# Two changes of order in a two-layer kernel: the weight folding among the experts, and a context product in the last two units

## The chip, the cores and the metric

The kernel runs on one core of a Trainium2 chip. The metric is the device time of one execution in microseconds (us); the median of the runs is what two kernels are compared by. The core has five engines with a queue each: TensorE (PE, with its weight loads shown as PEld), VectorE (DVE), ScalarE (ACT), GpSimd (POOL), and SyncE (SP), which here issues most of the transfers (DMAs). In what follows a line number such as L869 is a line of the kernel before.

## What is computed

Two layers over x of shape (4, 512, 512) in float32. Each adds to x an attention and a feed-forward part of the normed x:

```python
x = L0_attn_hidden_states
xn = _layernorm(x, axis=-1)
x = x + _L0_attn_ref(xn, ...) + _L0_ffn_ref(xn, ...)
xn = _layernorm(x, axis=-1)
x = x + _L1_attn_ref(xn, ...) + _L1_ffn_ref(xn, ...)
```

The change lies in the second layer alone. Its feed-forward part has four experts (E = 4); row n of a batch goes through expert n mod 4:

```python
x4 = x.reshape(B, G, E, H)
gu = jnp.einsum('bgeh,ehd->bged', x4, gate_up_proj)
gate, up = (gu[..., :I], gu[..., I:])
inter = jax.nn.silu(gate) * up
out = jnp.einsum('bgei,eih->bgeh', inter, down_proj)
```

Its attention works on compressed keys and queries, with 16 heads of 128 (H, D) and a rotation of half of each head:

```python
c_kv = hidden_states @ W_DKV + b_DKV
k = (c_kv @ W_UK + b_UK).reshape(b, s, H, D)
v = (c_kv @ W_UV + b_UV).reshape(b, s, H, D)
c_q = hidden_states @ W_DQ + b_DQ
q = (c_q @ W_UQ + b_UQ).reshape(b, s, H, D)
q_r = q @ W_QR
k_r = k @ W_KR
...
q = q.at[..., :RD].set(rope(q_r))
k = k.at[..., :RD].set(rope(k_r))
scores = jnp.einsum('bqhd,bkhd->bhqk', q, k) / jnp.sqrt(jnp.float32(D))
probs = jax.nn.softmax(scores, axis=-1)
ctx = jnp.einsum('bhqk,bkhd->bqhd', probs, v).reshape(b, s, H * D)
return ctx @ W_O + b_O
```

## The kernel before

**Order of instructions.** The program is written with tiles; a scheduler decides in which order the instructions of one engine stand, by the data that they need and by its own estimate of times. Each engine then works through its queue strictly in the order laid down, and waits where an instruction's data is not there. `tc.keep_in_program_order(ins)` adds an edge from the instruction that stands before it in the program on the same engine: the instruction can't be placed ahead of that one. In the attention's part nearly all instructions are held in this way, through a small helper `pin`.

**Stages.** The first layer fills the time up to some 976 us. Then come the four experts (to about 1150 us), and then the attention of the second layer in 64 units of one head and one batch.

**The experts (`hidden`, `returned`).** Expert e has a weight of 512 x 1024 for gate and up (`gu_e`, 2 MB) and one of 512 x 512 (`dn_e`). `hidden(e)` goes through four blocks of 128 columns. A block is done by products of 128 x 256 with fewer multiplications than the plain form (Strassen's scheme in Winograd's form): seven products, `a11`, `a12`, `s2`, `s1`, `s3`, `s4`, `a22`, of two matmuls each. They write into two tiles of PSUM, `epg` and `epu`. Three of the products go on adding to the same half of `epg`, called x, and ScalarE has to copy x out between them: L997 after `a11`, L999 after `s2`, L1003 after `s3`; L1001 copies `epu`. VectorE then makes the two sums `g` (tile `esg`: L1007 and L1008), ScalarE applies Silu to them (L1009), VectorE makes one more sum (L1010, tile `hold`) and the two products into `inter` (L1014). VectorE also makes the left operands of a later block from `gu` (L957 to L960, tile `s_ops`) and the right operands of the next expert (L946 to L949, tile `t_ops`). The copies share one tile, so the copy L997 of a block stands on ScalarE behind the Silu of the block before.

`gates(e)` loads `gu_e`; there are two buffers, and the load of `gu_2` waits until expert 0 has read `gu_0`. `returned(e)` multiplies `inter` with `dn_e` and adds to y (L1028, L1035).

**The folding (`fold`).** The rotation's matrices and the value projection are multiplied into the projections once for each group of four heads, by a generator that works in steps. It is run for group 0 among the experts and for groups 1 to 3 within the attention. A step i of it

- multiplies the transposed block of step i - 1 with W_QR or W_KR (`pw`, L864) and copies it to the weight (L865),
- transposes the loaded block on VectorE (`wt`, L869),
- loads the next block (`raw`, L875).

For group 0 `raw` and `wt` have one buffer each. The blocks are raw_0 to raw_4. At the end four products `pvo` (L882, copied by L883) make the folded output weight from rows `ow` of W_O (L855, two buffers), and VectorE sums these rows into `bo_part` (L886, L888). The first step, which only loads raw_0, is taken after expert 1's `hidden` in program order, one step in each block of experts 2 and 3, and one after expert 2. Called among the experts, `fold` gets no `pin`, and its default leaves every instruction to the scheduler:

```python
def fold(w, hg, wk, psum, bufs, pin=lambda ins: ins, ahead=1, rows=nc.sync):
```

**The attention's loop.** Unit i makes its queries and keys (`pk`, L1116, and `pq`, L1124, rotated on VectorE and GpSimd), the scores `sc` (L1134) and softmax of the unit before, whose probabilities are transposed on VectorE in blocks (`tt`, L1163) and set in place by 16 transfers (`prT`, L1194). The context product `pc` (L1202) is three units behind; ScalarE copies it to `ctxT` (L1204). When four heads of a batch have their context, the output product is made by seven products of Strassen's scheme again, split in four parts by a generator `outputs`:

- part 1: px = a11 b11, added to y
- part 2: p2 = a12 b21; px goes on with s2 t2; p2 and px are added to y
- part 3: p5 = s1 t1; px goes on with s3 t3; three additions to y
- part 4: p3 = s4 b22; px goes on with a22 t4; two additions to y, and for the last group the stores

px lies in one PSUM bank of its own; the next addition into it has to wait until VectorE has read the content before (L1266). p2, p5, p3, pk, pq and pc take turns in three banks (`ps_pj`). Of the 64 units one part is made in each; in the last turns of the loop (i = 63 and i = 64) two, because no unit comes after them. In the profile p2, p5 and p3 all have the name p. After the loop, `project_out` (L1302) makes the output of the last batch plainly, with the last two contexts `pc_next` and `pc_last` between.

The loop's part in question (i is the unit's number, nu is 64):

```python
for _ in range(1 if i < nu - 1 else 2):
    next(outs, None)
if i >= 3:
    hg, b, h = units[i - 3]
    context(probs.pop(i - 3), b, cs[hg, b], h, f"{i - 3}")
    if h == HPG - 1:
        outs = outputs(hg, b, ws[hg], cs[hg, b])
```

Of the kernel before, what the change touches and what calls it, by code (L numbers as in the profile page):

```python
# [55 lines left out]
def trunk_kernel(ctx: ExitStack, tc: tile.TileContext, a: dict, out: bass.AP):  # L56
    nc = tc.nc
# [48 lines left out]
    with ExitStack() as px:  # L106
        one = px.enter_context(tc.tile_pool(name="b_one", bufs=1))
        wk = px.enter_context(tc.tile_pool(name="b_wk", bufs=2))
# [10 lines left out]
        def psum():  # L119
            return ps_pj.tile([P, 512], F32, tag="pj", name="pj")  # L120
# [119 lines left out]
        k1, q1, rows = {}, {}, {}  # L240
# [582 lines left out]
    buq = lat.tile([P, H], F32, tag="b_UQ", name="b_UQ")  # L823
    lv = lat.tile([P, B, E, KVC], F32, tag="lv", name="lv")

# [14 lines left out]
        w["vo"] = pool.tile([P, HPG, HS], F32, tag="vo", name=f"vo_{hg}", bufs=1)  # L843
        return w

    def fold(w, hg, wk, psum, bufs, pin=lambda ins: ins, ahead=1, rows=nc.sync):

        heads = slice(hg * HPG, (hg + 1) * HPG)
        for nm, src in zip(ups, up_srcs):
            nc.sync.dma_start(out=w[nm][:, :, :RD], in_=src.rearrange("p (h d) -> p h d", h=H)[:, heads, :RD])  # L850
        raws, turned, ows = {}, {}, {}

        def output_rows(h):
            ows[h] = wk.tile([P, HS], F32, tag="ow", name=f"ow_{hg}_{h}", bufs=2)
            rows.dma_start(out=ows[h], in_=a["W_O"][(hg * HPG + h) * D : (hg * HPG + h + 1) * D, :])  # L855

        n = len(up_srcs)
        for i in range(n + 1 + ahead):
            k = i - ahead - 1
            if 0 <= k < n - 1:  # L860
                wt, wr, to = turned.pop(k), wqr if k else wkr, w[ups[k]]
                pw = psum(f"pw_{hg}_{i}").rearrange("p (h d) -> p h d", h=HPG)[:, :, :RD]
                for h in range(HPG):
                    pin(nc.tensor.matmul(pw[:, h, :], lhsT=wt[:, h, :], rhs=wr, start=True, stop=True))  # L864
                pin(nc.scalar.copy(to[:, :, RD:], pw))  # L865
            if 0 <= i - ahead < n:
                t = turned[i - ahead] = wk.tile([P, HPG, P], F32, tag="wt", name=f"wt_{hg}_{i - ahead}", bufs=1)
                pin(
                    nc.vector.transpose(  # L869
                        out=t.rearrange("p h c -> p (h c)"), in_=raws.pop(i - ahead).rearrange("p h c -> p (h c)")  # L870
                    )
                )
            if i < n:
                raw = raws[i] = wk.tile([P, HPG, P], F32, tag="raw", name=f"raw_{hg}_{i}", bufs=bufs)
                nc.sync.dma_start(out=raw, in_=blocks_d[i][:, heads, :])  # L875
            if i - n - ahead + 1 >= 0:
                output_rows(i - n - ahead + 1)
            yield
        wt = turned.pop(n - 1)
        for h in range(HPG):  # L880
            pv = psum(f"pvo_{hg}_{h}")
            pin(nc.tensor.matmul(pv, lhsT=wt[:, h, :], rhs=ows[h], start=True, stop=True))  # L882
            pin(nc.scalar.copy(w["vo"][:, h, :], pv))  # L883
            hh = hg * HPG + h
            if hh == 0:
                pin(nc.vector.tensor_scalar_mul(bo_part, ows[h], buv[:, :1]))  # L886
            else:
                pin(nc.vector.scalar_tensor_tensor(bo_part, ows[h], buv[:, hh : hh + 1], bo_part, ALU.mult, ALU.add))  # L888
            if h + 2 < HPG:
                output_rows(h + 2)  # L890
            if h == 1:
                yield
        if hg == NHG - 1:
            pb = psum("pbo")
            pin(nc.tensor.matmul(pb, lhsT=ones, rhs=bo_part, start=True, stop=True))
            pin(nc.vector.tensor_add(bo, pb, bo))

    with ExitStack() as px:
# [3 lines left out]
        wk = px.enter_context(tc.tile_pool(name="d_wk", bufs=2, reuse_waits="tile"))  # L902
# [181 lines left out]
    with ExitStack() as px:  # L1084
        wk = px.enter_context(tc.tile_pool(name="e_wk", bufs=2, reuse_waits="tile"))
# [1 line left out]
        ps_x = px.enter_context(tc.tile_pool(name="e_psx", bufs=1, space=PSUM))  # L1087
        ps_sc = px.enter_context(tc.tile_pool(name="e_pssc", bufs=4, space=PSUM))

        def pin(ins):  # L1090
            tc.keep_in_program_order(ins)
            return ins

        def rotate(t, ps, bias, trig, nm):

            mid = RD + HALF
# [118 lines left out]
        def rows_cols(t, qh, oh):  # L1215

            return t[:, 2 * qh : 2 * qh + 2, oh * half : (oh + 1) * half]

        def right_operands(w):
            vo, t = w["vo"], t_ops  # L1220
            b11, b12, b21, b22 = (vo[:, 2 * k : 2 * k + 2, o : o + half] for k in range(2) for o in (0, half))
            nc.gpsimd.tensor_sub(t[:, 0], b12, b11)
            nc.gpsimd.tensor_sub(t[:, 1], b22, t[:, 0])
            nc.gpsimd.tensor_sub(t[:, 2], b22, b12)
            nc.gpsimd.tensor_sub(t[:, 3], b21, t[:, 1])
            return dict(b11=b11, b21=b21, b22=b22, t1=t[:, 0], t2=t[:, 1], t3=t[:, 2], t4=t[:, 3])
# [28 lines left out]
        def outputs(hg, b, w, c):  # L1255

            if b == 0:
                ws_right[hg] = right_operands(w)
            r = ws_right[hg]

            def bank(pool, tag, nm):
                return pool.tile([P, 2, half], F32, tag=tag, name=f"{nm}_{hg}_{b}")

            def add(ps, qh, oh):
                t = rows_cols(y[b], qh, oh)
                pin(nc.vector.tensor_add(t, ps, t))  # L1266

            x = bank(ps_x, "px", "px")
            block_product(x, left_blocks(c)["a11"], r["b11"])
            add(x, 0, 0)  # L1270
            o = left_operands(c)
            yield
            p2 = bank(ps_pj, "pj", "p2")
            block_product(p2, o["a12"], r["b21"])
            block_product(x, o["s2"], r["t2"], False)
            add(p2, 0, 0)
            add(x, 0, 1)
            yield
            p5 = bank(ps_pj, "pj", "p5")
            block_product(p5, o["s1"], r["t1"])  # L1280
            block_product(x, o["s3"], r["t3"], False)
            add(p5, 0, 1)
            add(p5, 1, 1)
            add(x, 1, 1)
            yield
            p3 = bank(ps_pj, "pj", "p3")
            block_product(p3, o["s4"], r["b22"])
            block_product(x, o["a22"], r["t4"], False)
            add(p3, 0, 1)
            add(x, 1, 0)  # L1290
            if hg == NHG - 1:
                for e in range(E):
                    nc.sync.dma_start(out=rows_of(out, b)[:, e], in_=y[b][:, e])
            yield
# [23 lines left out]
        nu = len(units)  # L1318
        ws, cs, qk, probs = {}, {}, {}, {}
        folds, outs = iter(()), iter(())  # L1320
        ws[0] = w0
        for i in range(nu + 1):
            if i < nu:
                hg, b, h = units[i]
                if h == 0:
                    if b == 1 and hg + 1 < NHG:
                        ws[hg + 1] = group_tiles((lat, wk)[(hg + 1) % 2], hg + 1)
                        folds = fold(
                            ws[hg + 1],
                            hg + 1,  # L1330
                            wk,
                            lambda nm: ps_pj.tile([P, 512], F32, tag="pj", name=nm),
                            2,
                            pin,
                            2,
                            nc.gpsimd,
                        )
                        next(folds)
                    if i + HPG < nu:
                        cqs[units[i + HPG][:2]] = batch_latents(*units[i + HPG][:2])  # L1340
                    cs[hg, b] = wk.tile([P, HPG, L], F32, tag="ctxT", name=f"ctxT_{hg}_{b}")
                qk[i] = queries_keys(hg, b, h, ws[hg])
            if i == nu:
                last = list(probabilities(*qk.pop(i - 1), f"{i - 1}"))
            elif i == 1:
                head = list(probabilities(*qk.pop(0), "0"))
            elif i > 1:
                if i == 2:
                    probs[0] = turned_at_once(head, "head")
                probs[i - 1] = turn(softmax(*qk.pop(i - 1), f"{i - 1}"), f"{i - 1}")  # L1350
            for _ in range(1 if i < nu - 1 else 2):
                next(outs, None)
            if i >= 3:
                hg, b, h = units[i - 3]
                context(probs.pop(i - 3), b, cs[hg, b], h, f"{i - 3}")
                if h == HPG - 1:
                    outs = outputs(hg, b, ws[hg], cs[hg, b])
            if i % HPG != 0:
                next(folds, None)
            k = i - (nu - HPG * B)  # L1360
            if 0 <= k < HPG * B:
                b, e = divmod(k, HPG)
                nc.gpsimd.tensor_add(y[b][:, e, :], y[b][:, e, :], bo)
# [110 lines left out]
```

## Time and profile before

| what | value |
|---|---|
| median of 3 runs | 2060.4 us (2059.95 to 2061.85) |
| the profiled execution: time | 2058.69 us |
| its span, first to last instruction | 2056.9 us |
| TensorE busy, first layer (0 to 976 us) | 925.19 of 976.00 us |
| TensorE busy, experts (976 to 1150 us) | 160.58 of 174.00 us |
| TensorE busy, attention to unit 62 (1150 to 1994.8 us) | 838.37 of 844.80 us |
| TensorE busy, from unit 63 to the end (1994.8 to 2056.9 us) | 54.09 of 62.10 us |
| TensorE's granted clock in these four | 0.99, 0.96, 1.00, 0.97 |

The profile lists the instructions of one execution. A row of its view in order of time reads: start in us, busy us, engine, line, operation, out<-in, shapes, number of instructions (a matmul of float32 is listed as two); in brackets the idle time before it and what ended it. A row of its list of waits reads: engine and line that waited, what it waited for, us in total, number of times, longest. A row of a table by stretches of time reads: from:to, length, busy us (and number) of PE, PEld, DVE, ACT and POOL, the granted clock of TensorE (1.00 is full), the share of the DMA engines' time, GB/s.

### The profile page before, as it was taken

How to read it: one execution, taken by the hardware profiler on the slowest of the kernel's cores; microseconds unless marked ns; L12 is line 12 of the kernel's file. 1: busy time of each engine (PE TensorE's matmuls, PEld its weight loads, DVE VectorE, ACT ScalarE, POOL GpSimd, SP SyncE). 2: the span in 40 equal slices, each digit the busy share in tenths (PEclk: the TensorE clock that was granted, in tenths of full speed). 3: DMA queues.
4: the chain of work that ended last, by engine and by line, in shares of the span. 5: the costliest groups of instructions: out<-in, count | busy, mean ns of one | idle time of the engine just before them, and what ended most of it. 6: DMA issues, size and time to landing. Idle time of an engine off the chain costs nothing.

```text
span 2056.9 us, 30728 instructions
## 1 busy us (share of the span) xinstructions
PE 1978.2 (96%) x10502; PEld 1252.2 (61%) x10502; DVE 1301.4 (63%) x2720; ACT 866.9 (42%) x1765; POOL 588.6 (29%) x635
## 2 busy tenths in 40 slices
PE   8998999899999999998799999999999999999998
PEld 6776676767667776744677445555555555555554
DVE  5444666475755674744554487777777777777772
ACT  2233343334343443412222265555555555555552
POOL 5232333333332333320000132233223232344220
PEclk9999999999999999999899999999999999999999
DMA  6756566656364556663721144344434443333332
GB/s 165 207 147 180 132 193 156 169 142 186 116 186 126 157 172 169 196 200 117 262 73 56 46 105 115 91 113 110 108 94 114 102 114 89 94 96 94 99 91 82
DMA packets 338950, 270.89 MB, mean 132 GB/s; under 512 B 104043, under 2 KB 259884, under 8 KB 338156
## 3 DMA queue, kind: packets, MB, share of 16 engines
q1 hardware_dynamic: 323808, 254.36, 45.0%
q0 software_dynamic: 3488, 9.27, 1.4%
q10 hardware_dynamic: 11500, 5.32, 0.9%
q8 instruction: 84, 1.38, 0.3%
q14 instruction: 70, 0.57, 0.1%
HBM read 174.18 MB, written 34.87 MB: 102 GB/s over the span
## 4 chain that ended last, share of the span: by engine, by line
PE 45%; SPq 3%; DMA 2%; DVE 1%; ACT 1%; issue 0%; ACTq 0%; DVEq 0%
PE pc L1202 9%; PE sc L1134 9%; PE pq L1124 7%; PE px L1245 5%; PE p L1245 4%; PE epg L965 3%; PE epo L1028 3%; PE pk L1116 2%; SPq L1194 2%; PE epu L965 1%; PE po L1302 1%; PE pw L864 1%; PE pvo L882 1%; ACT prob L1139 1%; DMA y<-yd 1%
## 5 line engine op out<-in xcount | busy, mean ns | idle before, releaser
L1139 ACT ACTIVATE prob<-sc,mx 128x512 f32<-128x512 f32 x256 | 174.5, 684 | 160.7 <-DVE mx L1136 156.0
L1134 PE MATMUL sc<-kT,qT 96*128 96x512 f32 x512 | 230.6, 592 | 1.6 <-DVE prT_head L1183 1.3
L1202 PE MATMUL pc<-prT,lv 128*128 128x512 f32 x488 | 220.1, 594 | 0.7 <-DMA prT<-tt 0.7
L1163 DVE STREAM_TRANSPOSE tt<-prob 128x512 f32<-128x512 f32 x248 | 170.3, 706 | 55.1 <-ACT prob L1144 45.8
L1109 POOL TENSOR_TENSOR kT<-t_k,t_k 32x512 f32<-32x512 f32 x64 | 80.6, 1260 | 407.6 <-PE pq L1124 225.4
L117 PE MATMUL pf<-xT,wg 128*128 128x256 f32 x704 | 174.3, 390 | 13.5 <-DVE hid L478 7.3
L1144 ACT ACTIVATE prob<-prob,sm 128x512 f32<-128x512 f32 x256 | 176.6, 714 | 0.0
L1124 PE MATMUL pq<-cq,uq 128*128 128x512 f32 x384 | 175.3, 592 | 1.1 <-ACT ctxT L1204 1.1
L1134 PEld LDWEIGHTS sc<-kT,qT 96*128 96x128 f32 x512 | 96.8, 190 | 124.5 <-issue 119.4
L1136 DVE TENSOR_REDUCE mx<-sc 128x1 f32<-128x512 f32 x256 | 168.1, 677 | 6.2 <-PE sc L1134 4.2
L117 PE MATMUL pf<-xT,wu 128*128 128x256 f32 x704 | 170.4, 386 | 0.0
L117 PE MATMUL pd<-wd,hid 128*128 128x512 f32 x352 | 165.6, 600 | 1.0 <-DMA wd<-in_wd 0.7
L117 PEld LDWEIGHTS pf<-xT,wg 128*128 128x128 f32 x704 | 133.1, 193 | 39.9 <-DVE hid L478 9.4
L1202 PEld LDWEIGHTS pc<-prT,lv 128*128 128x128 f32 x488 | 92.8, 191 | 93.9 <-issue 89.6
L117 PEld LDWEIGHTS pf<-xT,wu 128*128 128x128 f32 x704 | 136.2, 194 | 19.6 <-issue 0.2
L478 DVE SCALAR_TENSOR_TENSOR hid<-pf,us,sg 128x256 f32<-128x256 f32 x88 | 41.7, 475 | 142.7 <-ACT sg L477 141.9
L1124 PEld LDWEIGHTS pq<-cq,uq 128*128 128x128 f32 x384 | 72.8, 190 | 93.4 <-issue 82.0
L314 POOL TENSOR_SCALAR sk<-k,m 128x256 f32<-128x256 f32 x64 | 61.0, 965 | 203.5 <-PE pz L117 190.4
L421 POOL TENSOR_SCALAR gh<-grad,m 128x256 f32<-128x256 f32 x64 | 62.6, 989 | 151.9 <-DVE grad L390 144.4
L117 PEld LDWEIGHTS pd<-wd,hid 128*128 128x128 f32 x352 | 63.6, 190 | 59.6 <-issue 44.8
L477 ACT ACTIVATE sg<-pf,gs 128x256 f32<-128x256 f32 x88 | 41.6, 474 | 131.7 <-PE pf L117 131.3
L1109 POOL TENSOR_TENSOR qT<-t_q,t_q 32x512 f32<-32x512 f32 x64 | 80.7, 1261 | 56.3 <-DVE t_q L1105 56.3
(301 smaller groups left out, 3512.2 us busy)
## 6 DMA issues: line engine op xcount, KB each, us to landing
prT<-tt SPq DMA_DIRECT2D x992, 64.0 KB, 2.0
wd<-in_wd SPq DMA_DIRECT2D x176, 256.0 KB, 3.0
wg<-in_wg SPq DMA_DIRECT2D x88, 256.0 KB, 2.8
wu<-in_wu SPq DMA_DIRECT2D x88, 256.0 KB, 3.2
cq<-lat_d SPq DMA_DIRECT2D x48, 256.0 KB, 3.9
rows<-rows SPq DMA_DIRECT2D x128, 66.0 KB, 2.2
kv<-rows SPq DMA_DIRECT2D x32, 264.0 KB, 4.3
gu<-in_gu SPq DMA_DIRECT2D x3, 2048.0 KB, 7.8
```

Source lines behind the costliest of these rows:

```text
L117: nc.tensor.matmul(out, lhsT=lhsT, rhs=rhs, start=start, stop=stop, skip_group_check=True)
L421: nc.gpsimd.tensor_scalar_mul(gh[:, :, h, :], g, m2[:, h : h + 1])
L965: nc.tensor.matmul(ps, lhsT=w[:, c, :], rhs=x[:, c], start=start and c == 0, stop=c == 1, skip_group_check=True)
L1109: nc.gpsimd.tensor_sub(t[RD:mid, :], t1[RD:mid, :], t2[RD:mid, :])
L1124: nc.tensor.matmul(pq, lhsT=w[f"uq{i}"][:, h, :], rhs=cqs[hg, b][:, i, :], start=(i == 0), stop=(i == nq - 1))
L1134: pin(nc.tensor.matmul(ps, lhsT=qT[:KQ, i * P : (i + 1) * P], rhs=kT[:KQ, :], start=True, stop=True))
L1136: pin(nc.vector.tensor_reduce(mx, ps, AX.X, ALU.max, negate=True))
L1139: pin(nc.scalar.activation(pr, ps, AF.Exp, bias=mx, scale=1.0, accum_out=sm))
L1144: pin(nc.scalar.mul(pr, pr, sm))
L1163: nc.vector.transpose(out=tt[:, :, :, i, :], in_=pr.rearrange("p (kb e j) -> p kb e j", e=2, j=K))
L1202: pin(nc.tensor.matmul(pc, lhsT=lv[:, b, k, :], rhs=prT[:, k, :], start=(k == 0), stop=(k == E - 1)))
L1245: nc.tensor.matmul(ps[:, q, :], lhsT=a[:, k, q * P : (q + 1) * P], rhs=w[:, k, :], start=start and k == 0 and q == 0, stop=k == 1, skip_gr ...
```

## The change

`pin` moves out of the attention's block to the start of the second layer, `fold` uses it always, and the parameter is gone. So the folding of group 0, among the experts, is kept in program order too. In the loop of units, the second of the two parts in the turns i = 63 and i = 64 is taken after the context product instead of before it.

```diff
@@ -823,6 +823,10 @@
     lv = lat.tile([P, B, E, KVC], F32, tag="lv", name="lv")
 
+    def pin(ins):
+        tc.keep_in_program_order(ins)
+        return ins
+
@@ -843,7 +847,7 @@
-    def fold(w, hg, wk, psum, bufs, pin=lambda ins: ins, ahead=1, rows=nc.sync):
+    def fold(w, hg, wk, psum, bufs, ahead=1, rows=nc.sync):
@@ -1087,10 +1091,6 @@
-        def pin(ins):
-            tc.keep_in_program_order(ins)
-            return ins
-
@@ -1331,7 +1331,6 @@
                             2,
-                            pin,
                             2,
                             nc.gpsimd,
@@ -1348,13 +1347,14 @@
-            for _ in range(1 if i < nu - 1 else 2):
-                next(outs, None)
+            next(outs, None)
             if i >= 3:
                 hg, b, h = units[i - 3]
                 context(probs.pop(i - 3), b, cs[hg, b], h, f"{i - 3}")
                 if h == HPG - 1:
                     outs = outputs(hg, b, ws[hg], cs[hg, b])
+            if i >= nu - 1:
+                next(outs, None)
```

## The prediction

> **What bounds the kernel now.** I read the totals first, then who waited for whom on TensorE, then the two places that came up in order of time on each engine, then the granted clock there.
>
> ```profile
> PE 1978.2 (96%) x10502; PEld 1252.2 (61%) x10502; DVE 1301.4 (63%) x2720; ACT 866.9 (42%) x1765; POOL 588.6 (29%) x635
> ```
>
> TensorE is busy nearly all the time, and the change adds and removes no matmul. It can only be worth the time in which TensorE waits or runs at a low clock. The waits of TensorE over the whole span hold two rows of lines that the change touches:
>
> ```profile
> PE epg L965 <- ACT hold L997: 12.4, 2, 11.4
> ...
> PE px L1245 <- DVE y L1266: 3.2, 1, 3.2
> ```
>
> The first is one wait of 11.4 us in expert 0, the second one wait of 3.2 us near the end. In order of time the first looks so, TensorE above, then ScalarE, then VectorE:
>
> ```profile
> 1001.65 1.03 PE L965 MATMUL epu<-t_ops,s_ops 128*128 128x256 f32 x4
> 1014.12 2.07 PE L965 MATMUL epg<-t_ops,s_ops 128*128 128x256 f32 x4 [11.44 <-ACT hold L997]
> 1015.98 1.91 PE L965 MATMUL epu<-xe,s_ops 128*128 128x256 f32 x4
> 1017.69 1.78 PE L965 MATMUL epg<-t_ops,gu 128*128 128x256 f32 x4
> 1019.30 1.03 PE L965 MATMUL epg<-xe,gu 128*128 128x256 f32 x4
> ```
> ```profile
> 1013.17 0.63 ACT L1009 ACTIVATE esg<-esg 128x512 f32<-128x512 f32 x1 [13.49 <-DVE esg L1007]
> 1013.71 0.35 ACT L997 COPY hold<-epg 128x256 f32<-128x256 f32 x1
> ```
> ```profile
> 999.72 0.43 DVE L1010 TENSOR_TENSOR hold<-hold 128x256 f32<-128x256 f32 x1 [0.49 <-ACT hold L1003]
> 1012.12 0.71 DVE L869 STREAM_TRANSPOSE wt<-raw 128x512 f32<-128x512 f32 x1 [11.98 <-DMA raw<-blocks_d]
> 1012.75 0.39 DVE L1007 TENSOR_TENSOR esg<-epg,hold 128x256 f32<-128x256 f32 x1
> ```
>
> The reader is to see a queue in order: VectorE stands 11.98 us at the folding's first transpose (wt_0), whose 256 KB (raw_0) are still on their way. Behind it waits the addition L1007 of expert 0, block 2; behind that ScalarE's Silu and the copy L997 for block 3; behind that TensorE. The fold's result is not needed before expert 2. After the wait three groups of products start 1.86, 1.71 and 1.61 us apart, where the same groups elsewhere start 0.86 us apart. The clock says why (second column the length, then busy times, then PEclk):
>
> ```profile
> 1002.70:1014.10 11.40, 0.00 (x0) 0.00 (x0) 1.28 (x3) 0.89 (x2) 0.00 (x0) 0.63 0.81 217
> 1014.10:1019.30 5.20, 5.18 (x12) 4.18 (x13) 3.03 (x8) 0.75 (x2) 0.00 (x0) 0.51 0.15 41
> ...
> 2005.40:2008.50 3.10, 0.01 (x1) 0.04 (x1) 2.41 (x6) 1.62 (x4) 0.00 (x0) 1.00 0.91 338
> 2008.50:2012.50 4.00, 4.00 (x10) 2.87 (x11) 1.33 (x2) 0.00 (x0) 0.00 (x0) 0.57 0.30 70
> ```
>
> The last two rows are the second place, unit 63:
>
> ```profile
> 2001.70 1.89 PE L1245 MATMUL px<-vo,ctxT 128*128 128x256 f32 x8
> 2003.43 1.89 PE L1245 MATMUL p<-vo,ctxT 128*128 128x256 f32 x8
> 2008.49 3.19 PE L1245 MATMUL px<-t_ops,s_ops 128*128 128x256 f32 x8 [3.17 <-DVE y L1266]
> 2011.48 4.10 PE L1202 MATMUL pc<-prT,lv 128*128 128x512 f32 x8
> ```
> ```profile
> 2006.44 1.32 DVE L1163 STREAM_TRANSPOSE tt<-prob 128x512 f32<-128x512 f32 x2 [0.45 <-ACT prob L1144]
> 2007.69 0.65 DVE L1266 TENSOR_TENSOR y<-px,y 128x512 f32<-128x512 f32 x1
> ```
>
> The second use of px must wait until VectorE has added its first content to y, and that addition stands behind the softmax's transposes. The context product pc, 3.4 us of ready work, stands behind the waiting matmul.
>
> **The change part by part.** The compiled orders of both kernels differ in two places only: the folding among the experts (where some sums of left operands also swap with a neighbour on VectorE), and the products of units 63 and 64. No instruction is added.
>
> *wt_0 moves.* It leaves expert 0, block 2 and comes to expert 1, block 2, between VectorE's L960 and L1010. TensorE's products after the wait can then start as in block 2: there L1007 started at 994.89 and the products 1.53 later, at 996.42, without idle time. In block 3, L1007 could start at 1000.95 (0.17 after its matmuls), so the copy is there at 1002.48; TensorE ends its earlier products at 1002.51 (1001.65 + 0.86). The start moves from 1014.12 to 1002.51: 11.61 us. Then three groups take 3 x 0.865 = 2.60 instead of 5.18 (1014.12 to 1019.30): 2.58 us. Together 14.2 us.
>
> Its new place costs 0.71 us of VectorE. It starts at about 1038.15 by the old times, L1010 slips from 1038.65 to some 1038.8, and L1007 behind it has 0.84 us of idle time to lose: nothing. Its data landed at about 1012 and are needed at 1024 (1038 less 14). If that cover were gone, the same wait would return there.
>
> *raw_1 moves on SP* behind the load of gu_2 (expert 2's weights) and buv. It waits for wt_0 (raw has one buffer); behind it stands gu_3, which needs expert 1's end at 1046.12 - 14.2 = 1031.9 anyway; raw_1 is gone by 1026. Nothing.
>
> *What is late next: gu_2.* It is issued at 1021.23 now, when expert 0 ends; then at about 1009, as soon as SP is through with ow_1. Its first reader, L957, comes at 1035.57 - 14.2 = 1021.4. Alone the 2 MB took 7.8 us from issue to landing; behind other loads y's 1 MB took up to 15.7 us. So landing lies between 1016.8 and 1024.7. The reader has 0.6 us of VectorE idle time behind it, so the cost is 0 to 2.7 us, and 1.7 more if the clock drops for one stretch of 3.4 us. I take 0, by the nearer row (same transfer, and only about 1 MB is still ahead of it at 1009).
>
> *wt_1 to wt_3, the pw products and copies.* In expert 2 the transposes move behind L1014, where VectorE is idle 0.65 us before L957 (1067.67); they take 0.71: 0.06 us late, and the addition after next waits 0.51 us for TensorE. wt has one buffer and so has raw: each load is issued up to 2.9 us later (1067.8 for 1064.9) and is needed at 1073.95, 6.2 us on; these loads took 2.9 us. The pw products (0.84 us) leave the place behind L1003's copy; the two first products of the next block (0.86) fill it instead. The copies of pw go behind the Silu: 0.37 us between its end at 1066.23 and the next copy at 1066.86, so 0.26 us of room. Nothing, with 0 to 0.3 us for each of three blocks as bounds.
>
> *Expert 3.* The bo_part sums move behind block 0 and block 1. So ow_2 is issued at about 1111.05 instead of 1109.43 and lands 2.6 us later, ow_3 at some 1115.3; their products move back to 1117.0 and 1117.9. Nothing.
>
> *Unit 63.* pc moves ahead of p. px ends 2003.43, pc (prT_60 was issued before 1990) 2006.87, p 2008.60. The addition to y ends 2008.34 as before, so the second px starts at 2008.60 without wait and at full clock, and the scores of unit 63 follow at 2010.33 instead of 2015.41: 5.08 us. ScalarE's copy of pc finds its engine free at 2007.0. If the wait came back, VectorE's row allows a start at 2008.49, so no more than 0.1 us is at stake.
>
> *Unit 64.* There TensorE has no wait now, from 2015.41 to 2048.4; pc only changes place with p3 and px. p3's sum and px's sum come 3.4 us later in this order, but po's first two banks are older ones, and the banks that wait for these sums are used 3.4 us and more after 2024.1. Nothing. The rest (po, the last context, the last sums and stores) moves as one.
>
> Sum: 14.2 + 5.1 = 19.3 us. The profiled execution took 2058.69 us (2056.9 of span and 1.8 around it), so it would take 2039.4; it lay 1.7 us under the median of the three runs, 2060.4, so the forecast for the median is **2041.1 us**.
>
> [...]
>
> **The rivals.**
>
> *1. gu_2 comes late.* For it: about 9 MB are on the queue between 979 and 1013. Against: by 1013 DMA traffic had died down. Price at most 2.7 + 1.7 = 4.4: 2045.5. Chance 0.07.
>
> *2. The low clock in unit 63 has another cause and stays.* Then 5.1 shrinks to the wait alone, 3.2: 2043.0. Chance 0.07; the 2.39 us gap speaks against it.
>
> *3. wt_0's wait was for something other than raw_0* (its semaphores cover several loads) and appears again in expert 1. Then only the end gains: 2060.4 - 5.1 = 2055.3. Chance 0.05; the transpose starts right at a landing of raw_0.
>
> *4. Slower: the single raw buffer.* In expert 2 each of three loads now starts only after VectorE's L1014 and the transpose, and VectorE stops at the next transpose until it lands, with TensorE behind it as in expert 0. It costs from the point where a load takes over 6.2 us. At y's 15.7 us each would cost 9.5: 28.5 - 19.3 = 9.2 slower, 2069.6; over 12.6 us each it is slower than before. Against: these loads took 2.9 us, and DMA moves next to nothing from 1056 to 1064. Chance 0.04.
>
> **How the numbers follow.** The forecast has 0.77, its own range 2038 to 2043.5 (the three runs spread 1.9 us, the small bounds add about 1). The range for 8 in 10 reaches over rivals 1 and 2: 2037.5 to 2046. A run of this kernel can be told from no change at about 0.2%, 4 us. Forecast and rivals 1 and 2 are all faster by more, rival 3 by 5.1, just over it: faster 0.95, same 0.01, slower 0.04.
>
> **What would show it.** In expert 0: no wait of VectorE at L869, the block 3 products about 1.5 us after L1007, PEclk 1.00; wt_0 in expert 1 without idle time before it. At the end: px's second use without a wait, PEclk 1.00, the scores of unit 63 right behind. A wait at L957 on the load of gu_2 would be rival 1, a wait at wt_1 to wt_3 rival 4. The forecast is wrong if either gap stays in another place.

## The result: 0.991 of the time before

| | before | changed |
|---|---|---|
| median | 2060.18 us (4 runs, 2056.9 to 2061.85) | 2042.65 us (4 runs, 2040.5 to 2044.78) |
| ratio | | 0.991, 95% interval 0.9897 to 0.9922 |

The two profiled executions, cut at the starts of instructions: the first matmul into epg, the first into pk, unit 63's into pk, and the end of the span.

| stretch, us | before | changed | difference |
|---|---|---|---|
| first layer, to the first epg | 978.37 | 983.49 | +5.12 |
| experts, to the first pk | 180.29 | 166.13 | -14.16 |
| attention, to unit 63's pk | 836.17 | 836.33 | +0.16 |
| unit 63 to the end | 62.07 | 57.04 | -5.03 |
| span | 2056.90 | 2042.98 | -13.92 |

The change touches the second and fourth rows, and these give 19.2 us. The first layer's instructions stand in the same order in both kernels; its time scatters from one execution to the next, as the part on the prediction shows.

In order of time the changed kernel, first TensorE at expert 0, block 3 (columns as before: start, busy, then in brackets idle time and its end; lines L826 to L1089 of the kernel before are four higher here, so L1011 is the old L1007, L873 the old L869 and L1001 the old L997):

```profile
1006.76 1.03 PE L969 MATMUL epu<-t_ops,s_ops 128*128 128x256 f32 x4
1007.63 1.03 PE L969 MATMUL epg<-t_ops,s_ops 128*128 128x256 f32 x4
1008.49 1.08 PE L969 MATMUL epu<-xe,s_ops 128*128 128x256 f32 x4
1009.40 1.03 PE L969 MATMUL epg<-t_ops,gu 128*128 128x256 f32 x4
```

ScalarE and VectorE at the same place:

```profile
1006.56 0.63 ACT L1013 ACTIVATE esg<-esg 128x512 f32<-128x512 f32 x1 [1.76 <-DVE esg L1011]
1007.10 0.35 ACT L1001 COPY hold<-epg 128x256 f32<-128x256 f32 x1
```
```profile
1004.83 0.42 DVE L1014 TENSOR_TENSOR hold<-hold 128x256 f32<-128x256 f32 x1 [0.50 <-ACT hold L1007]
1006.10 0.42 DVE L1011 TENSOR_TENSOR esg<-epg,hold 128x256 f32<-128x256 f32 x1 [0.84 <-PE epg L969]
...
1026.52 0.42 DVE L961 TENSOR_TENSOR s_ops<-gu 128x256 f32<-128x256 f32 x1
...
1029.03 0.70 DVE L873 STREAM_TRANSPOSE wt<-raw 128x512 f32<-128x512 f32 x1
```

No bracket at 1007.63: the products that waited 11.44 us start 1.53 us after L1011. VectorE goes from L1014 to L1011 and waits there for TensorE alone. wt_0 comes 23 us behind this L1011, without idle time ahead of it, and L961, the first reader of gu_2, does not wait for its load. The end, TensorE in unit 63:

```profile
1992.82 1.89 PE L1245 MATMUL px<-vo,ctxT 128*128 128x256 f32 x8
1994.54 3.60 PE L1202 MATMUL pc<-prT,lv 128*128 128x512 f32 x8
1997.98 1.89 PE L1245 MATMUL p<-vo,ctxT 128*128 128x256 f32 x8
1999.70 1.89 PE L1245 MATMUL px<-t_ops,s_ops 128*128 128x256 f32 x8
2001.43 3.60 PE L1134 MATMUL sc<-kT,qT 96*128 96x512 f32 x8
```

and VectorE's addition that the second px needs:

```profile
1998.80 0.65 DVE L1266 TENSOR_TENSOR y<-px,y 128x512 f32<-128x512 f32 x1
```

The addition is done at 1999.45, when TensorE is still at p: the context product covers the wait, with 0.25 us to spare before the second px at 1999.70. From unit 63's pk (1985.95) the scores come after 15.48 us; before it was 20.58 (1994.83 to 2015.41). In the table by stretches (length, busy us of the five engines, PEclk, DMA share, GB/s) the clock is full at both places:

```profile
1006.00:1011.90 5.90, 5.90 (x29) 5.00 (x28) 4.62 (x11) 2.01 (x5) 0.00 (x0) 1.00 0.66 136
...
1999.70:2004.90 5.20, 5.20 (x18) 3.08 (x18) 3.61 (x7) 1.60 (x5) 0.00 (x0) 1.00 0.36 83
```

### The profile page after: what moved, and what is told of

It reads as the page before. It is cut to its first block, busy times and chain, and to the rows that moved or that the text cites. A ratio compares the mean times of both kernels' runs of the same rounds, so it can differ in the third digit from the quotient of the medians.

```text
span 2043.0 us, 30727 instructions
## 1 busy us (share of the span) xinstructions
PE 1976.8 (97%) x10502; PEld 1253.0 (61%) x10502; DVE 1303.0 (64%) x2720; ACT 865.8 (42%) x1765; POOL 587.6 (29%) x635
## 4 chain that ended last, share of the span: by engine, by line
PE 48%; DVE 1%; ACT 1%; SPq 1%; issue 0%; DMA 0%; DVEq 0%; ACTq 0%
PE pc L1202 10%; PE sc L1134 10%; PE pq L1124 8%; PE px L1245 5%; PE p L1245 4%; PE epg L969 3%; PE epo L1032 3%; PE pk L1116 3%; PE epu L969 1%; PE po L1302 1%; PE pw L868 1%; PE pvo L886 1%; SPq L1194 1%; ACT prob L1139 0%; ACT prob L1144 0%
```

## The experiments

Expectations count "experts" and "unit 63 to the end" as in the table above. All were written before the run. Where no median is given, the experiment stands on one profiled execution.

### One part of the change at a time

The folding alone is the changed kernel with the old loop:

```diff
-            next(outs, None)
+            for _ in range(1 if i < nu - 1 else 2):
+                next(outs, None)
...
-            if i >= nu - 1:
-                next(outs, None)
```
The loop alone is the kernel before with the new loop:

```diff
-            for _ in range(1 if i < nu - 1 else 2):
-                next(outs, None)
+            next(outs, None)
...
+            if i >= nu - 1:
+                next(outs, None)
```

> The folding is kept in program order, the loop of units stays as before. My theory: all of the 14.2 us among the experts and nothing at the end. From the first product of the experts to the first pk: 166.1 us (before 180.3). From unit 63's pk to the end: 60 to 62.1 us (before 62.1, of which up to 1.9 hang on how the clock falls). Time about 2046. Rival (the two parts are worth something only together): less than 10 us.

> Only the loop of units is changed, the folding is placed as before. My theory: the experts' stretch stays at 180.3 us with the 11.4 us wait and PEclk near 0.5 after it; unit 63 to the end takes 57.0 us (before 62.1). Time about 2055. Rival (the low clock in unit 63 has its own cause): 58.9 us and a stretch at half clock there.

| | experts | unit 63 to the end | median | ratio to before, 95% |
|---|---|---|---|---|
| folding alone | 166.16 | 62.40 | 2046.77 | 0.9929 (0.9913 to 0.9946) |
| loop alone | 181.09 | 56.78 | 2055.40 | 0.9973 (0.9962 to 0.9984) |

The kernel before, run beside these, had a median of 2061.13 us (13 runs). The parts add up: each shows its own gain and none of the other's.

### Which instruction of the folding

Only the transposes kept in order, against the kernel before:

```diff
-                pin(
+                tc.keep_in_program_order(
                     nc.vector.transpose(
```
All but the transposes of group 0, against the changed kernel with the old loop:

```diff
-                pin(
+                (pin if hg else lambda ins: ins)(
                     nc.vector.transpose(
```
The first transpose of group 0 alone, against the kernel before:

```diff
-                pin(
+                (pin if hg or i > ahead else tc.keep_in_program_order)(
                     nc.vector.transpose(
```

> The kernel before with only the five transposes of the first folding kept in program order; its matmuls, copies and sums are placed freely. My theory (the first transpose is the whole cause): experts 166.1 us, no wait of VectorE at a transpose of the first folding. Rival (the matmuls and copies must be kept as well): 170 us or more.

> The folding kept in program order except the transposes of the first folding, which stand where they stood before; the loop of units as before. My theory: the wait of about 12 us of VectorE at the first transpose is back, experts 180 us, PEclk about half after it. Rival (products and copies count): 175 us or less.

> The kernel before with a single instruction kept in program order, the first folding's first transpose. My theory: this alone gives the whole gain among the experts, 166.1 us. Rival (the later transposes and products count): 167 us or more.

Experts: 166.14 with the transposes kept, 180.47 with all but the transposes kept, 166.14 with the first transpose alone kept. The list of waits (what waited, for what, us, times, longest) of the kernel in which all but the transposes are kept, first VectorE, then TensorE:

```profile
DVE wt L873 <- DMA raw<-blocks_d: 12.2, 1, 12.2
```
```profile
PE epg L969 <- ACT hold L1001: 12.7, 2, 11.7
```

And TensorE's in the kernel with one instruction kept:

```profile
PE epg L965 <- ACT hold L997: 1.0, 1, 1.0
PE epu L965 <- DVE t_ops L946: 1.0, 1, 1.0
```

The wait follows the transpose: in all six executions in which it stands in expert 0, TensorE waits 10.6 to 12.1 us, and the wait is gone when the transpose alone is held back. In the kernel with one instruction kept, the order differs from before in the place of this transpose and of the load of raw_1, which waits for it, and in nothing else. The many other edges do nothing to the experts' time.

### Load the block earlier instead

Against the kernel before, the folding's first step is taken as soon as the folding is set up:

```diff
                 first = fold(w0, 0, wk, lambda nm: psp.tile([P, 512], F32, tag="pa", name=nm), 1)
+                next(first)
...
-            if e in (1, 2):
+            if e == 2:
                 next(first, None)
```

> The kernel before with the first step of the folding (the loads of uk, uq and raw_0) taken ahead of the loads of b_UK, b_UQ, trig and ckv, nothing kept in order. The scheduler then puts the first transpose one block earlier (expert 0, block 1). My theory (the wait is the landing less the place in the queue): raw_0 lands some 5 us earlier and the place is 5 us earlier too, so VectorE waits 9 to 12 us there, TensorE's wait is ahead of block 2, experts 177 to 181 us. Rival (the load's late issue is the cause): the wait shrinks by 5 us or more, experts 174 us or less.

Experts took 179.81 us. From the experts' start (983.78) raw_0 was issued after 22.6 us instead of 27.5, and wt_0 started after 26.85 us instead of 33.75. But the scheduler had put it a block further ahead, and VectorE met it 5.4 us earlier:

```profile
999.71 0.41 DVE L960 TENSOR_TENSOR s_ops<-gu,s_ops 128x256 f32<-128x256 f32 x1
1010.63 0.71 DVE L869 STREAM_TRANSPOSE wt<-raw 128x512 f32<-128x512 f32 x1 [10.50 <-DMA raw<-blocks_d]
```

A load that comes 7 us earlier bought 1.5 us of the wait. Both times the scheduler set the transpose 10 to 12 us ahead of the landing; that its own estimate of the landing does this was not tested.

### The wait and the clock in unit 63

Products that nobody reads fill the gap, against the kernel before:

```diff
             block_product(p2, o["a12"], r["b21"])
+            if hg == NHG - 1 and b == B - 2:
+                idle = ps_sc.tile([P, L], F32, tag="sc", name="idle")
+                for k in range(E):
+                    pin(nc.tensor.matmul(idle, lhsT=lv[:, b, k, :], rhs=ckv[:, b, :], start=(k == 0), stop=(k == E - 1)))
             block_product(x, o["s2"], r["t2"], False)
```

> The kernel before, with four products of 128x512 that nobody reads (3.43 us of TensorE) between p2 and the second use of px in unit 63, where TensorE waited 3.17 us. It does more work. My theory (the low clock comes from TensorE's idle time): the second use of px starts at once after the filler and takes 1.73 us, the context product 3.43, so the scores of unit 63 come about 1.5 us earlier than before measured from unit 63's pk (19.0 us instead of 20.6), and unit 63 to the end takes about 60.5 us (before 62.1). Rival (the half clock has its own cause): it is there as before, the scores come at 20.6 us or later and the end is 62.1 us or longer.

Its TensorE in order of time:

```profile
2009.74 3.60 PE L1278 MATMUL idle<-ckv,lv 128*128 128x512 f32 x8
2013.17 1.89 PE L1245 MATMUL px<-t_ops,s_ops 128*128 128x256 f32 x8
2014.90 3.60 PE L1202 MATMUL pc<-prT,lv 128*128 128x512 f32 x8
2018.33 3.60 PE L1134 MATMUL sc<-kT,qT 96*128 96x512 f32 x8
```

More work in the same gap, and the scores come at 18.91 us from unit 63's pk instead of 20.58, at a granted clock of 1.00 from 2013.20 to 2018.30; unit 63 to the end took 60.27 us. By itself this one execution does not prove that idle time brings the half clock, as the six executions of the old loop without the filler show that the same gap of 3.17 us does not always bring it. With the early load it did not, with one instruction kept it did (table by stretches, the gap and what follows; the early load first):

```profile
2010.30:2013.50 3.20, 0.03 (x2) 0.03 (x1) 2.51 (x6) 1.73 (x4) 0.00 (x0) 1.00 0.89 330
2013.50:2017.00 3.50, 3.50 (x12) 2.36 (x13) 1.34 (x2) 0.00 (x0) 0.00 (x0) 1.00 0.34 80
```
```profile
1994.70:1997.80 3.10, 0.00 (x0) 0.01 (x1) 2.41 (x6) 1.66 (x4) 0.00 (x0) 1.00 0.91 339
...
1998.90:2002.30 3.40, 3.40 (x8) 2.01 (x7) 0.69 (x1) 0.00 (x0) 0.00 (x0) 0.50 0.39 91
```

In all, the half clock followed in five of the six executions with the gap, and in none of the seven without it (the filler, and six with the context product ahead), which speaks for idle time as its cause. Unit 63 to the end took 60.35 us with the early load, and 62.06 to 62.40 in the five others. Of the 5.0 us at the end, 3.3 are the wait and 0 or 1.7 to 2.0 the clock.

### Unit 63 and turn 64 apart

Against the kernel before:

```diff
-            for _ in range(1 if i < nu - 1 else 2):
+            for _ in range(2 if i == nu else 1):
                 next(outs, None)
...
+            if i == nu - 1:
+                next(outs, None)
```

> The kernel before with the context product ahead of part 2 in unit 63, and the order of turn 64 as before. My theory: all of the gain at the end is here, unit 63 to the end 57.0 us. Rival (turn 64's order counts): 58 us or more.

56.89 us: turn 64's new order is worth nothing, as there was no wait in it.

### Two loads made late

raw_0 three times, against the changed kernel:

```diff
-                nc.sync.dma_start(out=raw, in_=blocks_d[i][:, heads, :])
+                for _ in range(3 if hg == i == 0 else 1):
+                    nc.sync.dma_start(out=raw, in_=blocks_d[i][:, heads, :])
```
raw_2 and raw_3 three times, against the changed kernel:

```diff
-                nc.sync.dma_start(out=raw, in_=blocks_d[i][:, heads, :])
+                for _ in range(3 if hg == 0 and i in (2, 3) else 1):
+                    nc.sync.dma_start(out=raw, in_=blocks_d[i][:, heads, :])
```

> The changed kernel, but raw_0 is loaded three times in a row, which holds SP and so the load of gu_2 back by some 6.4 us. It tests the prediction's first rival. By the changed kernel's trace gu_2 is issued 31.5 us after the experts' first product and read at 43.0; with 6.4 us more and 7.8 us to landing it comes at 45.7. My theory: VectorE waits 2 to 4 us at the first L961 on gu_2, experts 168 to 171 us. Rival (gu_2 has more room): 166.1 us.

> The changed kernel, but the loads of raw_2 and raw_3 are done three times each, one after the other, so that each takes some 9.7 us instead of 3.2. It tests the price in the prediction's fourth rival: such a load has 6.2 us. My theory: VectorE waits 3 to 4 us at the transposes of raw_2 and raw_3 and TensorE with it, experts 171 to 175 us (changed kernel 166.1). Rival (there is more room than that): experts 166 to 168 us.

With raw_0 loaded three times, gu_2 was issued 37.7 us after the experts' start instead of 31.5, and VectorE met its first reader (L962 in this kernel, which has one line more above it):

```profile
1031.67 0.43 DVE L962 TENSOR_TENSOR s_ops<-gu 128x256 f32<-128x256 f32 x1 [3.27 <-DMA gu<-in_gu]
```

Experts took 167.87 us. The wait is as expected; the cost of 1.74 us misses the expected range from below, since part of the wait was covered: TensorE itself stood 1.49 us. How much gu_2 has to spare in the changed kernel stands in that kernel's own trace: it lands 9.6 us after its issue, 41.05 us from the experts' start, and is read at 43.03, so 2.0 us. Issued 6.2 us later it was read at 46.40, at most 8.7 us after its issue, so its landing moved by less than its issue.

With raw_2 and raw_3 loaded three times, VectorE did wait, but nothing came of it: experts 166.13 us, and TensorE shows the two waits of 1.0 us alone that it has without.

```profile
1064.12 0.71 DVE L873 STREAM_TRANSPOSE wt<-raw 128x512 f32<-128x512 f32 x1 [1.11 <-DMA raw<-blocks_d]
1074.16 0.71 DVE L873 STREAM_TRANSPOSE wt<-raw 128x512 f32<-128x512 f32 x1 [2.53 <-DMA raw<-blocks_d]
```

The expectation missed. The two transposes come 10.0 us apart here and 6.9 in the changed kernel. Kept in program order means not ahead of the instruction before, but the scheduler may still place them later. In the compiled order they stand three and seven places further back on VectorE, where the wait costs TensorE nothing. So what 9.4 us of load would cost at the old place was not measured.

### The two edits that matter

The kernel before with the first transpose kept in order and the call moved in unit 63, and nothing else of the change:

```diff
-                pin(
+                (pin if hg or i > ahead else tc.keep_in_program_order)(
                     nc.vector.transpose(
...
-            for _ in range(1 if i < nu - 1 else 2):
+            for _ in range(2 if i == nu else 1):
                 next(outs, None)
...
+            if i == nu - 1:
+                next(outs, None)
```

> The kernel before with two edits: the first folding's first transpose is kept in program order, and in unit 63 the context product comes ahead of part 2. My theory: all of the changed kernel's gain, experts 166.1 us, unit 63 to the end 57.0 us, time 2041 to 2043. Rival (the rest of the change adds something): 2 us or more above that.

Median 2041.74 us (4 runs; the kernel before, run beside it, 2060.51 in 7), ratio 0.9902 (0.988 to 0.9923), experts 166.14, unit 63 to the end 57.24. One edge on one transpose and one moved call are all of the gain.

## Why the prediction was right, and what was off

**wt_0, 14.2 us:** 14.16 measured, and the path was the one told: transpose, L1007, Silu, copy, products, clock. Keeping that transpose alone gives all of it. That the size agrees to 0.04 us is in part luck: with the transpose at its old place the experts took 180.29 to 181.09 us in five executions, so the gain is 14.2 to 15.0. The third rival, a wait for something other than raw_0, did not come: at its new place the transpose starts without idle time.

**Its new place, the later transposes, the copies of pw, raw_1, expert 3, at nothing:** right as a whole. The experts took 166.13 us with all of these moved and 166.14 with only the first transpose kept.

**gu_2 at nothing:** right, though its load was mis-sized. The prediction went by 7.8 us from issue to landing; the changed kernel's took 9.6, while a load issued before it was still on its way (rows of W_O landed 3.8 us after gu_2's issue). The reader came where it was forecast, 43.0 us from the experts' start, and 2.0 us were left. Made later, the load becomes the next wait (3.27 us with raw_0 loaded three times), as the first rival says.

**Unit 63, 5.08 us:** 5.03 measured. But it was told as a fixed sum, and its clock part is not fixed: in one of six executions of the old loop it was missing, and the gain would have been 3.3 us. That the profile before had the low clock was likely (five of six), not certain. The second rival gave the low clock another cause; the filler and the six executions with the context product ahead speak against it. The gap of 2.39 us that it names is TensorE's from 49.80 to 52.19 in the profile before; the half clock followed from 53.23 to 56.64.

**Unit 64 at nothing:** right.

**The fourth rival's point, 6.2 us a load:** not settled. Loads of 9.4 us cost nothing, but they changed the placing too, so the forecast place was not tried.

**The term that was off is the base.** The forecast was 2041.1, the median 2042.65, though both gains were met to 0.05 us. The sum was set against the median of three runs, 2060.4, as if the rest of the time stood still. In 13 profiled executions, all with the first layer's instructions in one order, the first layer took 978.4 to 985.3 us, and the profile that the forecast was read from was the shortest of them. These 6.9 us of scatter are more than the second gain, and what makes them was not found. The miss of 1.6 us is small beside the 4.3 us that the four runs of the changed kernel spread; the prediction had counted with the 1.9 us of its three runs.

## What to carry to other kernels

Look at the head of each in-order queue: a single instruction whose data is late, and whose result nobody needs yet, stops all that stands behind it, however idle its engine is on average (here wt_0, for 11.98 us, on a VectorE that is busy 63% of the span). Hold back that one instruction; an earlier load helps little where a scheduler moves the instruction ahead with it (7 us earlier bought 1.5 us). Where a short wait of TensorE can be covered by ready work from further down its queue, count the clock behind the gap as a bonus that some executions do not pay (here 1.7 to 2.0 us in five of six, nothing in the sixth). Where the part that the change doesn't touch scatters by more than the gain (6.9 us against 5.0 at the end), measure the change in its own stretch.

## What the runs showed of the hardware

In the traces of the kernel before and the changed one the stretches at half clock are 3.41 or 6.83 us long, but for one of 13.65 us (1005.55 to 1019.20), which begins in the wait of 11.44 us in expert 0, and for the last of each trace, which begins at 2056.86 and 2041.66 us and reaches to the span's end. Within each trace they begin a whole number of 3.413 us apart (before: 53.23, 176.11 and 2009.07, the second 36 such steps after the first, the third 537 after the second).

The length of a gap alone does not tell whether the half clock follows. In the kernel before, the gap of 2.39 us from 49.80 was followed by it, from 53.23 to 56.64, and one of 2.11 us that ended at 504.29 was not (table by stretches, each gap and what follows):

```profile
49.80:52.20 2.40, 0.01 (x1) 0.01 (x1) 2.26 (x7) 1.49 (x2) 2.03 (x5) 1.00 0.26 39
53.30:56.60 3.30, 3.30 (x10) 2.56 (x9) 0.27 (x1) 0.00 (x0) 0.00 (x0) 0.50 0.06 8
502.20:504.30 2.10, 0.01 (x1) 0.01 (x1) 2.00 (x6) 0.00 (x0) 2.10 (x3) 1.00 1.04 398
504.30:509.00 4.70, 4.70 (x22) 4.16 (x23) 2.42 (x6) 1.75 (x4) 2.41 (x3) 1.00 0.66 216
```

In the first layer of the changed kernel 1.67 us of idle time within the 3.41 us from 437.40 (68 short matmuls) were followed by the half clock, from 440.81 to 444.22. The gap of 3.17 us in unit 63 was followed by it in the kernel before (0.50 from 2009.07 to 2012.48, with 2.83 us of the gap in the 3.41 us just ahead) and with one instruction kept (0.50 from 1998.90 to 2002.30), but not with the early load (1.00 from 2013.50 to 2017.00). What else than idle time counts, these runs do not show.
